# The ffn's base product by Strassen's scheme on two levels instead of one

## The chip, the cores and the metric

The kernel runs on one core of a Trainium2 chip. The metric is the device time of one execution in microseconds (us); a lower time is better. All data are float32.

## The reference

A transformer block for 32 sequences of 64 tokens, D = 1024. The parts with adapters are cut to what matters:

```python
x = x + attn(cond(x))               # cond: x @ W.T + a rank-32 adapter chosen by sequence
x = x + ffn(cond2(x))               # attn: 32 heads, 8 key/value heads, rotary, causal, w_o
def cond2(x):                       # 8 experts of rank 16, top 2
    return x @ W.T + 2 * experts2(x)
def ffn(y):                         # 8 experts of rank 16, top 2
    return y @ W_base.T + b_base + 2 * experts3(y)
```

Nothing nonlinear stands between the two dense products of cond2 and ffn but their gates, so the kernel multiplies the weights together once: the ffn's *base* is one product of x (1024 by 2048 tokens) with a combined matrix "cf" (1024 by 1024) that the kernel makes itself from W_base and cond2's W.

## The kernel before

Everything is kept transposed: features lie in the 128 partitions, tokens in the free dimension. Every large product is made by Strassen's scheme with Winograd's sums: a product of 2 x 2 blocks by seven block products `p1` to `p7` instead of eight. The class `Group` makes one such product for a pair of output chunks of 128 features. Its weights are three blocks of w ("11", "12", "22") and four sums s1 to s4 that GpSimd makes (`weight_sums`); its right sides are blocks of x and four sums t1 to t4 that VectorE makes (`column_sums`). Three PSUM banks x, y, z collect the seven products: p1 is copied out by ScalarE and then p2 goes on top in x, p6 and then p7 and p4 share y, p5 and then p3 share z; VectorE adds the parts on the way out. `mult` issues the matmuls of one product: 4 of 512 columns for a K half of 512.

The work goes in this order:

1. The *gen* stage makes the combined matrices: cq and ckv (kept in the scratch `cqkv`), then cf. For cf, `multiply("cf", ...)` goes through four groups; each makes four tiles of 128 x 512 that ScalarE's queue stores to the scratch `cffn`. Between its steps, a table `after` has other work done: the narrow columns (`narrow`), the rows of b2 (`low_rows`), and the sums of the attention's output weights w_o, which go to the scratch `wos`.
2. For each half `hf` of the tokens (1024): q and k, attention, the output projection, then the ffn.
3. The ffn: logits (`lgrows`, `lg`), gates, a product `h` for the experts' inner parts, the scaled inner parts `hw2` and `hw3`, and the base in four groups `ffn_pair(g)`. The experts' outer parts are added in PSUM: in the first group by `extra` (8 matmuls), in the others by one more matmul in each of the seven products (`tail`, over the sums `bs` and `th`).

In the gen stage the order on SP (loads), TensorE and VectorE is as written (`manual_schedule`, closed by `in_order.close()`); afterwards a scheduler orders the engines, but for parts that are marked again. Buffers come from pools: `wp` with two buffers each for the tags "w" (128 x 8 KB, a group's weights, `load_w` at line 404) and "s" (their sums), `tp` with eleven temporaries of 128 x 512, PSUM with three banks "bank" and five "ps". A tile's load waits until all that read the buffer's last tenant have finished.

```python
wp = ctx.enter_context(tc.tile_pool(name="wp", bufs=2))
tp = ctx.enter_context(tc.tile_pool(name="tp", bufs=11))
```

Of the kernel before, what the change touches and what calls it, by code (L numbers as in the profile page):

```python
# [76 lines left out]
def block_kernel(ctx: ExitStack, tc: tile.TileContext, a, out: bass.AP):  # L77
# [94 lines left out]
    def weight_sums(w, name, s=None):  # L172

        h = w.shape[1] // 2
        a11, a12 = w[:, :h, :P], w[:, h:, :P]
        a21, a22 = w[:, :h, P:], w[:, h:, P:]
        if s is None:
            s = wp.tile([P, 4, h, P], F32, tag="s", name=f"s_{name}")
        nc.gpsimd.tensor_add(s[:, 0], a21, a22)  # L179
        nc.gpsimd.tensor_sub(s[:, 1], s[:, 0], a11)  # L180
        nc.gpsimd.tensor_sub(s[:, 2], a11, a21)
        late["sums"] = nc.gpsimd.tensor_sub(s[:, 3], a12, s[:, 1])
        return s
# [34 lines left out]
    def columns(name, pool, b, n, h=H):  # L218
        tiles = [pool.tile([P, h, 512], F32, tag=f"sum{j}", name=f"sum{j}_{name}") for j in range(4)]
        return Columns(b, n, h, [[t[:, kc, :] for kc in range(h)] for t in tiles])  # L220
# [8 lines left out]
    class Group:  # L229
# [4 lines left out]
        def __init__(self, name, w, s, t, out, extra=None, known=None, bank=group_bank, late=False):  # L234
            self.name, self.out, self.extra, self.known, self.late = name, out, extra, known, late
            self.n, self.b, self.new = t.n, t.b, bank
            h = self.h = w.shape[1] // 2
            self.weights = {"11": w[:, :h, :P], "12": w[:, h:, :P], "22": w[:, h:, P:]}
            for j in range(4):
                self.weights[f"s{j + 1}"] = s[:, j]  # L240
# [13 lines left out]
        tail = None  # L254

        def mult(self, ps, left, right, first=False):
# [9 lines left out]
            if self.tail is not None:  # L266
                lhs, rhs = self.tail(left, right)
                nc.tensor.matmul(ps, lhs, rhs, start=False, stop=True, skip_group_check=True)
# [73 lines left out]
        def without_extra(self):  # L342

            for step in (self.p1, self.p6, self.p5, self.p7, self.p2, self.p4):
                step()

        def with_extra(self):
            self.more(self.z, 1, 1)
            self.out11()
            self.out00()  # L350
            self.p3()
            self.out10()
# [118 lines left out]
    cffn = scratch.tile([P, KC, NF], F32, tag="cffn", name="cffn")  # L471
    b1q = const.tile([P, NQ], F32, tag="b1q", name="b1q")
# [9 lines left out]
    with tc.tile_pool(name="gen", bufs=1) as gen:  # L482
# [56 lines left out]
        def multiply(name, inner, t, n, dst, at, diagonal=False, first=(), order=None, after={}):  # L539

            h = n // 2
            ws, groups = list(first), {}

            def load(g):
                while len(ws) <= min(g, 3):
                    ws.append(load_w(a[inner][len(ws)], f"{name}{len(ws)}"))

            def out(g, r, c, ps, add):
                o = tmp(f"{name}{g}{r}{c}")[:, :h]
# [4 lines left out]
                if diagonal and r == c:  # L554
                    d = o[:, g * P : (g + 1) * P]
                    nc.vector.tensor_add(d, d, ident)
                nc.scalar.dma_start(dst[:, g + r * H, at + c * h : at + (c + 1) * h], o)
# [112 lines left out]
        b2 = gen.tile([P, KC, P], F32, tag="w_os", name="b2")  # L670
        nc.sync.dma_start(b2, a["b2"])
        low_rows("b2f0", b2, w3, 512, b2s)

        def narrow(g, w):
            for r in range(2):
# [8 lines left out]
                nc.scalar.dma_start(cffn[:, g + r * H, D:], o)  # L684

            for n in range(2 * g, 2 * g + 2):
# [6 lines left out]

        multiply(
            "cf", "w2", t_cf, D, cffn, 0, diagonal=True,
            after={
                (0, "p1"): lambda w: low_rows("b2x", b2, w3x, NF - D, b2s[:, D:]),
                (0, "p7"): lambda w: low_rows("b2f1", b2, w3[:, :, 512:], 512, b2s[:, 512:]),
                (0, "p3"): lambda w: narrow(0, w),
                (1, "p4"): lambda w: narrow(1, w),  # L700
                (2, "p4"): lambda w: narrow(2, w),
                (3, "p4"): lambda w: narrow(3, w),
            },
        )

# [56 lines left out]
    def scaled(n, hf, h, gates):  # L762

        nm = f"r{n}_{hf}"
        both = hp.tile([P, TH], F32, tag="hw", name=f"hw{nm}")
        hw = [both[:, s * 512 : (s + 1) * 512] for s in range(NS)]
        for s in range(NS):
# [9 lines left out]
            nc.vector.tensor_mul(hw[s], h[s], gs)  # L777
# [5 lines left out]
    for hf in range(2):  # L783
# [15 lines left out]
        else:  # L799
# [3 lines left out]
            with tc.issue_after(late["third"].ins):  # L803
                tiles = [
                    gathered(hf, s, lambda name: a1[:, s * BS : (s + 1) * BS], BS) for s in range(NS)
                ]
            steps = [ranks(hf, s, x, tiles[s], low) for s in range(NS)]
# [30 lines left out]
        def qk_pair(g, z_bank=group_bank):  # L838
            w = load_w(cqkv[:, :, g * WG : (g + 1) * WG], f"qk{hf}{g}")
# [217 lines left out]
        with tc.manual_schedule():  # L1057
# [98 lines left out]
            xt = columns(f"y{hf}", scoped(f"sums_y{hf}", side="right"), x_half, 512)  # L1156
# [17 lines left out]
        bd = fp.tile([P, 2, P], F32, tag="bd", name=f"bd_{hf}")  # L1174
        bs = fp.tile([P, 4, 3, P], F32, tag="bs", name=f"bs_{hf}")
        th = fp.tile([P, 4, 512], F32, tag="th", name=f"th_{hf}")
        for kc in range(2, H):
            xt.make(kc)
        lg = ps_tile(f"lg_{hf}")
        for c in range(2):  # L1180
# [11 lines left out]
            nc.scalar.copy(rs, rows)  # L1192
            for i in range(4):
# [8 lines left out]
        lgv = lg[:, : NT * 2 * E].rearrange("p (t n e) -> p t n e", n=2, e=E)  # L1202
        lg3 = small(f"lg3_{hf}")
        nc.vector.tensor_copy(lg3, lgv[:, :, 1, :])
        gates2 = gates_of("2", hf, lgv[:, :, 0, :], lbias[:, hf * NT : (hf + 1) * NT, :])
# [14 lines left out]
        Group(f"h{hf}", w, weight_sums(w, f"h{hf}"), xt, out_h).early()  # L1220


        b2v, b3v = (b[:, :D].rearrange("p (g r o) -> p g r o", r=2, o=P) for b in (b2f, b3))
        for i, b in enumerate((b2v, b3v)):
            nc.gpsimd.tensor_sub(bd[:, i], b[:, 0, 0], b[:, 0, 1])
        nc.gpsimd.tensor_add(bs[:, 0], b2v[:, 1:, 1], b3v[:, 1:, 1])
        nc.gpsimd.tensor_sub(bs[:, 1], bs[:, 0], b2v[:, 1:, 0])
        nc.gpsimd.tensor_sub(bs[:, 2], b2v[:, 1:, 0], b2v[:, 1:, 1])
        nc.gpsimd.tensor_sub(bs[:, 3], b3v[:, 1:, 0], bs[:, 1])

        def ffn_pair(g):
            w = load_w(cffn[:, :, g * WG : (g + 1) * WG], f"f{hf}{g}")

            def out_f(r, c, ps, add):
                oc = 2 * g + r
                o = tmp(f"o_{hf}_{oc}_{c}")
                if add is None:
                    nc.scalar.activation(o, ps, AF.Identity, bias=bb[:, oc : oc + 1])
                else:
                    nc.vector.scalar_tensor_tensor(o, ps, bb[:, oc : oc + 1], add, ALU.add, ALU.add)  # L1240
                nc.scalar.dma_start(out[oc, :, hf, c, :], o)

            def extra(r, c):
                if (r, c) == (0, 1):
                    return [(bd[:, 0], hw2[1]), (bd[:, 1], hw3[1])]
                return [(b2v[:, 0, r], hw2[c]), (b3v[:, 0, r], hw3[c])]

            def tail(left, right):
                lhs = {"11": b2v[:, g, 0], "12": b3v[:, g, 0], "22": b3v[:, g, 1]}
                rhs = {"11": hw2[0], "21": hw3[0], "22": hw3[1]}  # L1250
                return (
                    bs[:, int(left[1]) - 1, g - 1] if left[0] == "s" else lhs[left],
                    th[:, int(right[1]) - 1] if right[0] == "t" else rhs[right],
                )

            s = weight_sums(w, f"f{hf}{g}")
            if g == 0:
                return Group(f"f{hf}{g}", w, s, xt, out_f, extra, late=True)
            group = Group(f"f{hf}{g}", w, s, xt, out_f)
            group.tail = tail  # L1260
            return group

        hw2 = scaled("2", hf, [h[0, c] for c in range(2)], gates2)
        ps = ps_tile(f"lgx_{hf}")
        for t in range(NT):
            nc.tensor.matmul(
                ps[:, t * E : (t + 1) * E],
                hw2[t // 4][:, t % 4 * P : (t % 4 + 1) * P],
                b2f[:, NF - E :],
                start=True,  # L1270
                stop=True,
            )
        gates3 = gates_of("3", hf, ps[:, : NT * E].rearrange("p (t e) -> p t e", e=E), lg3)
        for c in range(2):
            ps = ps_tile(f"hx_{hf}_{c}")
            nc.tensor.matmul(ps, b2f[:, D : D + P], hw2[c], start=True, stop=True)
            nc.vector.tensor_add(h[1, c], h[1, c], ps)
        first = ffn_pair(0)
        first.without_extra()
        hw3 = scaled("3", hf, [h[1, c] for c in range(2)], gates3)  # L1280
        first.with_extra()
        column_sums([th[:, j] for j in range(4)], lambda i, c: (hw2, hw3)[i][c], lambda t: t)
        for g in range(1, 4):
            group = ffn_pair(g)
            if g == 2:
                late["third"] = late["sums"]
            group.main()
# [89 lines left out]
```

## Time and profile before

| | us |
|---|---|
| median of 3 runs | 1213.21 (1212.85 to 1213.22) |
| the profiled execution | 1213.1 |
| its span, first to last instruction | 1211.3 |
| TensorE busy | 1203.2 |
| VectorE busy | 577.9 |
| GpSimd busy | 511.4 |
| ScalarE busy | 153.4 |

PE is TensorE's matmuls, PEld its weight loads, DVE VectorE, ACT ScalarE, POOL GpSimd, SP the engine that issues most loads; SPq and ACTq are DMAs issued there. A float32 matmul of the code appears as two records with a weight load each. A line such as `662.47 3.43 PE f_y L258 x8` of the chain reads: start, duration, engine, tile, line of the code, number of records. In the groups, "busy, mean ns | idle before, releaser" follow the shapes; a mean matmul record of 592 ns includes the drain, which overlaps the next one. Line 258 is `mult`, line 268 the `tail`, line 876 the v projection.

The stages by time: gen to about 296 us (cf from 176), q and k of the first half to 430, attention to 590, the ffn of the first half to 748, then the second half to 1211.

### The profile page before, as it was taken

The page shows a single profiled execution, that of the slowest core. Times are in us where ns is not written, and L with a number is a line of the kernel's source. Part 1 is how long each engine was busy: PE and PEld are TensorE (multiplying, and loading weights), DVE is VectorE, ACT ScalarE, POOL GpSimd, SP SyncE. Part 2 cuts the span into 40 slices and gives each one's busy share as a digit, 9 for nine tenths or more (in the row PEclk, how much of TensorE's full clock was granted, in tenths as well). Part 3 has the DMA queues.
Part 4 walks back from the last instruction along what each step waited for, and adds up shares of the span by engine and source line. Part 5 has one row for each costly group of instructions (what it writes and reads, how often), then busy time and mean ns, then how long its engine had stood idle before and what let it go on. Part 6 is the DMA issues. An engine that isn't in the chain of part 4 may idle for free.

```text
span 1211.3 us, 13619 instructions
## 1 busy us (share of the span) xinstructions
PE 1203.2 (99%) x5440; PEld 611.9 (51%) x5440; DVE 577.9 (48%) x941; ACT 153.4 (13%) x282; POOL 511.4 (42%) x437
## 2 busy tenths in 40 slices
PE   9999999999999999999999999999999999999998
PEld 3444874555444478544444444444468544444443
DVE  4312151115357789753941113456789764842111
ACT  1001000000001124320000000000224330000000
POOL 3341351443434746754723411532756653821010
PEclk9999999999999999999999999999999999999999
DMA  6553742645111111023112435111120124112110
GB/s 244 211 214 99 263 144 61 204 160 166 35 35 35 36 70 71 17 73 123 36 35 83 126 109 169 35 35 35 35 71 32 40 71 126 50 35 69 56 50 35
DMA packets 58992, 108.83 MB, mean 90 GB/s; under 512 B 5168, under 2 KB 35248, under 8 KB 57648
## 3 DMA queue, kind: packets, MB, share of 16 engines
q1 hardware_dynamic: 43136, 79.53, 19.7%
q10 hardware_dynamic: 13104, 20.03, 4.5%
q0 software_dynamic: 2688, 8.39, 2.1%
q8 instruction: 43, 0.70, 0.2%
q14 instruction: 21, 0.17, 0.0%
HBM read 83.72 MB, written 24.22 MB: 89 GB/s over the span
## 4 chain that ended last, share of the span: by engine, by line
PE 98%; DMA 1%; SPq 0%; DVE 0%; issue 0%
PE qk_y L258 9%; PE o_y L258 7%; PE f_y L258 7%; PE qk_x L258 6%; PE qk_z L258 6%; PE v L876 5%; PE f_z L258 5%; PE o_x L258 5%; PE f_x L258 5%; PE o_z L258 5%; PE cq_y L258 3%; PE cf_y L258 3%; PE sc L897 3%; PE pt L950 2%; PE cq_z L258 2%; PE cf_z L258 2%
## 5 line engine op out<-in xcount | busy, mean ns | idle before, releaser
L826 POOL TENSOR_TENSOR raw<-raw,consts 128x512 f32<-128x512 f32 x40 | 63.0, 1584 | 105.7 <-DVE t L825 105.7
L930 POOL TENSOR_TENSOR e<-e,top 128x512 f32<-128x512 f32 x64 | 64.9, 1042 | 57.3 <-DVE top L929 42.2
L942 POOL TENSOR_TENSOR e<-e,tot 128x512 f32<-128x512 f32 x64 | 66.1, 1064 | 27.3 <-DVE tot L940 27.3
L258 PE MATMUL qk_x<-x,w_qk 128*128 128x512 f32 x160 | 72.2, 594 | 0.0
L258 PE MATMUL qk_y<-sum_x,s_qk 128*128 128x512 f32 x160 | 72.2, 594 | 0.0
L179 POOL TENSOR_TENSOR s_f<-w_f 128x512 f32<-128x512 f32 x8 | 11.0, 1373 | 122.3 <-DMA w_f<-cffn 79.9
L258 PE MATMUL o_x<-q,w_o 128*128 128x512 f32 x128 | 58.9, 592 | 0.0
L876 PE MATMUL v<-w_v,x 128*128 128x256 f32 x256 | 58.7, 382 | 0.0
L258 PE MATMUL f_x<-x,w_f 128*128 128x512 f32 x128 | 57.9, 592 | 0.0
L258 PE MATMUL f_y<-sum_y,s_f 128*128 128x512 f32 x128 | 57.5, 592 | 0.0
L1051 POOL TENSOR_TENSOR x<-x,o_u 128x512 f32<-128x512 f32 x24 | 30.9, 1289 | 54.3 <-DVE o_u L1049 33.2
L876 PEld LDWEIGHTS v<-w_v,x 128*128 128x128 f32 x256 | 47.4, 190 | 8.4 <-issue 2.7
L258 PEld LDWEIGHTS qk_x<-x,w_qk 128*128 128x128 f32 x160 | 30.1, 190 | 38.0 <-issue 37.9
L827 DVE TENSOR_TENSOR t<-t,consts 128x512 f32<-128x512 f32 x40 | 48.7, 1230 | 0.7
L258 PEld LDWEIGHTS qk_y<-sum_x,s_qk 128*128 128x128 f32 x160 | 30.2, 190 | 37.1 <-issue 36.4
L179 POOL TENSOR_TENSOR s_qk<-w_qk 128x512 f32<-128x512 f32 x10 | 19.5, 1947 | 65.8 <-DMA w_qk<-cqkv 65.8
L939 DVE TENSOR_REDUCE tot<-e 128x8 f32<-128x512 f32 x64 | 40.5, 667 | 10.6 <-ACT e L934 10.4
L934 ACT ACTIVATE e<-e 128x512 f32<-128x512 f32 x64 | 38.2, 639 | 54.3 <-POOL e L930 54.2
L920 DVE TENSOR_TENSOR e<-sc,consts 128x512 f32<-128x512 f32 x64 | 39.7, 676 | 8.9 <-PE sc L897 8.9
L258 PEld LDWEIGHTS f_y<-sum_y,s_f 128*128 128x128 f32 x128 | 24.3, 190 | 30.6 <-issue 30.6
L258 PEld LDWEIGHTS f_x<-x,w_f 128*128 128x128 f32 x128 | 24.3, 190 | 30.6 <-issue 30.6
L836 DVE TENSOR_TENSOR q<-raw,t 128x512 f32<-128x512 f32 x32 | 38.4, 1205 | 2.5 <-POOL raw L826 2.3
(321 smaller groups left out, 2207.6 us busy)
## 6 DMA issues: line engine op xcount, KB each, us to landing
w_qk<-cqkv SPq DMA_DIRECT2D x10, 1024.0 KB, 5.5
x<-in_xT SPq DMA_DIRECT2D x16, 512.0 KB, 8.0
w_o<-in_wo SPq DMA_DIRECT2D x16, 512.0 KB, 4.7
s_o<-wos SPq DMA_DIRECT2D x16, 512.0 KB, 6.3
w_f<-cffn SPq DMA_DIRECT2D x8, 1024.0 KB, 5.5
outT<-o ACTq DMA_DIRECT2D x32, 256.0 KB, 2.9
cqkv<-cq ACTq DMA_DIRECT2D x16, 256.0 KB, 2.4
w_ckv<-in_w SPq DMA_DIRECT2D x4, 1024.0 KB, 5.4
```

Source lines behind the costliest of these rows:

```text
L258: nc.tensor.matmul(ps, self.weights[left][:, kc, :], self.right(right, kc), start=first and kc == 0, stop=kc == self.h - 1, skip_group_che ...
L826: nc.gpsimd.tensor_mul(rv, rv, c3)
L827: nc.vector.tensor_mul(t2v, t2v, s3)
L836: nc.vector.tensor_add(*unfinished.pop())
L876: nc.tensor.matmul(begun[t], x[kc][:, t * P : (t + 1) * P], wv[:, kc, :], start=False, stop=kc == KC - 1, skip_group_check=True,)
L897: nc.tensor.matmul(sc[j][:, n * S : (n + 1) * S], q[rows, g, b, 2 * mp : 2 * mp + 2, :].rearrange("p m t -> p (m t)"), k[rows, g, b, :], s ...
L920: nc.vector.tensor_add(per_key(e), per_key(sc[j]), mask.unsqueeze(1).to_broadcast([P, 8, S]))
L930: nc.gpsimd.tensor_sub(ev, ev, wide(top))
L934: nc.scalar.activation(e, e, AF.Exp, scale=SCALE)
L939: nc.vector.tensor_reduce(tot[:, i], es[i], AX.X, ALU.add)
L942: nc.gpsimd.tensor_mul(es[i], es[i], wide(tot[:, i]))
L1051: nc.gpsimd.tensor_add(xo, xo, to)
```

## The change

Each of the seven products of the base is itself made by seven products of *quarters*. Where the base was four groups with 512 x 512 blocks split once, it is now seven outer products (table `SEVEN`), each in two quarters (q = 0, 1), each quarter a `Quarter(Group)` with K halves of 256 (two matmuls a product) and 256 columns.

- The weights' sums of both levels are made once, in the gen stage, and kept in a scratch `cf7`: for each outer product seven blocks for each kappa (half of K) and q. A quarter loads its 14 blocks of 128 x 128 in one DMA into the tag "w". GpSimd's weight sums in the ffn's base are gone.
- cf's four groups run in the order 0, 2, 1, 3 of the output chunks and stay in SBUF (tile `cf`). `levels(kappa)` makes eleven steps (`level_one`: one of the outer sums, `level_two`: the inner sums of one outer block and its five stores on SP). Those of kappa 0 stand between the steps of the third group, on VectorE; those of kappa 1 after the last group, on VectorE and, for three blocks, on GpSimd.
- In the ffn the columns' inner sums (`inner_columns`) are made by VectorE in the tag "s". The outer level is added outside PSUM in accumulators a, b, c, z of 128 x 4 x 512: GpSimd adds the earlier accumulator to a quarter's parts (`known`), VectorE adds the result on the way out of PSUM.
- The experts' outer parts are now extra matmuls of 256 columns, eight in each quarter of p2, p5, p3 and p4. `tail`, `bs` and `th` are gone.
- The order on TensorE in the ffn is as written: of each quarter `begin` (p1, p6), then `finish` of the quarter before (p4, p3), then `middle` (p5, p2, p7, out11). The logits' second part, the gates' transposes and the `h` product are interleaved in a new order.
- In the gen stage the rows of b2 for columns 0 to 1023 move from before and inside cf to after it, the w_o sums are spread over cf's steps, the first qk weights are loaded inside cf, and the gathers for the second half are tied to two additions of GpSimd.

```diff
+    class Quarter(Group):
+        def sum(self, x):
+            if x != "u1":
+                self.pair = tmp(f"{self.name}_{x}")
+            at = self.n if x == "u1" else 0
+            return self.pair[:, at : at + self.n]
+        def begin(self):
+            self.p1()
+            self.p6()
+        def middle(self):
+            for step in (self.p5, self.p2, self.p7, self.out11):
                 step()
+        def end(self):
+            self.p4()
             self.p3()
+    SEVEN = (
+        *(("p1", "11", "11"), ("p6", "s2", "t2"), ("p2", "12", "21"), ("p7", "s3", "t3")),
+        *(("p5", "s1", "t1"), ("p3", "s4", "22"), ("p4", "22", "t4")),
+    )
+    PRIOR = {"p6": "a", "p2": "a", "p7": "b", "p3": "b", "p4": "c"}
+    KEPT = {"p1": "a", "p6": "b", "p7": "c", "p5": "z"}
+    OUT = {"p2": (0, 0), "p3": (0, 1), "p4": (1, 0), "p5": (1, 1)}
...
+    cf7 = scratch.tile([P, 7, 2, 2, 7, P], F32, tag="cf7", name="cf7")
...
+        def level_two(kappa, left, x, engine):
+            n = at_of[left]
...
+            engine.tensor_add(s[0][:, :, 0], a21, a22)
+            engine.tensor_sub(s[0][:, :, 1], s[0][:, :, 0], a11)
+            engine.tensor_sub(s[1][:, :, 0], a11, a21)
+            engine.tensor_sub(s[1][:, :, 1], a12, s[0][:, :, 1])
+            to = cf7[:, n, :, kappa]
+            for at, block in enumerate((a11, a12, a22)):
+                nc.sync.dma_start(to[:, :, at, :], block)
+            for i in range(2):
+                nc.sync.dma_start(
+                    to[:, :, 3 + 2 * i : 5 + 2 * i].rearrange("p q s o -> p q (s o)"),
+                    s[i].rearrange("p q s o -> p q (s o)"),
+                )
...
-        b2 = gen.tile([P, KC, P], F32, tag="w_os", name="b2")
+        b2 = hp.tile([P, TH], F32, tag="hw", name="b2").rearrange("p (k o) -> p k o", o=P)
         nc.sync.dma_start(b2, a["b2"])
-        low_rows("b2f0", b2, w3, 512, b2s)
...
+        for half in range(2):
+            at = slice(half * 512, (half + 1) * 512)
+            low_rows(f"b2f{half}", b2, w3[:, :, at], 512, b2s[:, at])
+        for step in levels(1, nc.gpsimd):
+            step()
...
+        def quarter(n, q):
+            step, _, _ = SEVEN[n]
+            w = wp.tile([P, KC, WG], F32, tag="w", name=f"w_f{hf}{n}{q}")
+            w = w.rearrange("p k o -> p (k o)")[:, : 14 * P].rearrange("p (k s o) -> p k s o", k=2, s=7)
+            nc.sync.dma_start(w, cf7[:, n, q])
...
+            def known(m, half, add):
+                if prior is not None:
+                    to = part(prior if kept is None else kept, m, half)
+                    late["sum"] = nc.gpsimd.tensor_add(to, part(prior, m, half), add)
...
-        for g in range(1, 4):
-            group = ffn_pair(g)
-            if g == 2:
-                late["third"] = late["sums"]
-            group.main()
+            for n in range(7):
...
+                for q in range(2):
...
+                    group = quarter(n, q)
+                    group.begin()
+                    if last is not None:
+                        finish(last)
+                    group.middle()
+                    if q == 0 and n < 6:
+                        ts[n + 1] = inner_columns(n + 1)
+                    last = group
...
+            finish(last)
```

## The prediction

> **What bounds the kernel now.** I read the page first: the engines' busy times and the chain that ended last.
>
> ```profile
> PE 1203.2 (99%) x5440; PEld 611.9 (51%) x5440; DVE 577.9 (48%) x941; ACT 153.4 (13%) x282; POOL 511.4 (42%) x437
> PE 98%; DMA 1%; SPq 0%; DVE 0%; issue 0%
> ```
>
> TensorE is busy in 99% of the span and is 98% of the chain; every other engine is at half or less. A matmul removed from the ffn is worth its full length, and every wait put on TensorE costs its full length. So I need two prices: a product, and a wait for weights. Next the chain in order of time, in the ffn of the first half, and in the v stage, which has matmuls of 256 columns.
>
> ```profile
> 662.47 3.43 PE f_y L258 x8
> 666.76 3.43 PE f_z L258 x8
> 671.05 3.43 PE f_y L258 x8
> ...
> 434.94 3.46 PE v L876 x16
> ```
>
> A matmul of the code gives two records. Four matmuls of 512 columns take 3.43 us, 0.858 us each; the next product starts 4.29 us after this one, and the 0.86 between is the tail (one matmul for the experts). Eight matmuls of 256 columns take 3.46 us, 0.4325 us each, so half the columns cost 50.4%. The groups by form show why weight loads don't spoil that:
>
> ```profile
> L876 PE MATMUL v<-w_v,x 128*128 128x256 f32 x256 | 58.7, 382 | 0.0
> L876 PEld LDWEIGHTS v<-w_v,x 128*128 128x128 f32 x256 | 47.4, 190 | 8.4 <-issue 2.7
> ```
>
> Two weight loads of 190 ns are 380 of the 432 ns. Last, SP's waits and the timeline around one weight load of the ffn:
>
> ```profile
> SPq L404 <- PE f_y L258: 167.1, 6, 39.9
> ...
> 615.58 3.70 PE L258 MATMUL h_y<-sum_y,w_h 128*128 128x512 f32 x8
> 619.11 3.60 PE L258 MATMUL h_z<-x,s_h 128*128 128x512 f32 x8
> 619.35 0.52 SPq L404 DMA_DIRECT2D w_f<-cffn  x1
> 624.97 1.51 POOL L179 TENSOR_TENSOR s_f<-w_f 128x512 f32<-128x512 f32 x1 [17.16 <-DMA w_f<-cffn]
> ...
> w_f<-cffn SPq DMA_DIRECT2D x8, 1024.0 KB, 5.5
> ```
>
> A load waits at SP until TensorE has done with the buffer's last tenant: the next product starts at 619.11, the load is issued at 619.35, its 1 MB is there 5.5 us later, its reader starts 0.12 after that. Nobody waits on TensorE, because the other of the two buffers holds a whole group, 7 x 4.29 = 30 us of work.
>
> **What the Trainium skill says.** "DMA: Bandwidth & Descriptors", section "Anatomy of one DMA", gives about 2.0 us plus bytes over 436 GB/s: 4.4 us for 1 MB. The trace has 5.4 to 5.8 (another queue than the page's fit), so I use the trace. "TensorE: Matmul & The Clock Gate", section "HAM oscillation", warns of idle gaps over about 3.4 us, after which the clock halves; in this trace the granted clock is 0.999 and there are no such gaps in the ffn. "SBUF — State Buffer", section "Who interferes with whom", says that VectorE operations with two SBUF inputs and GpSimd's reads shut each other out. The trace agrees: the same four sums beside GpSimd and without it are
>
> ```profile
> 165.13 5.58 DVE L191 TENSOR_TENSOR sum_cf<-w 128x512 f32<-128x512 f32 x4
> 170.64 2.48 DVE L193 TENSOR_TENSOR sum_cf<-w,sum_cf 128x512 f32<-128x512 f32 x4
> ```
>
> **The change, part by part.**
>
> *TensorE's work.* Before, per half: four groups x 28 matmuls plus 8 extras and 21 tails = 141 x 0.858 = 121.0 us (trace: 622.1 to 748.2 less about 5 us of small gate matmuls). After: 14 quarters x 14 = 196 matmuls of 256 columns, and 8 quarters (those of p2, p5, p3, p4) x 8 extras = 64: 260 x 0.4325 = 112.45 us. Saved: 8.6 per half, **17.1 us** in all.
>
> *The wait for weights.* The pool of w keeps two buffers. Quarter i+2 takes the buffer of quarter i, whose last reader is p3 in `finish`, and `finish(i)` stands behind `begin(i+1)`. What TensorE still has before `begin(i+2)` is then only: the two extras of p3 of i if it has extras (0.86 us), the six matmuls of `middle(i+1)` (2.60), and its four extras if it has them (1.73). So the cover is 2.60 to 5.19 us where it was some 30.
>
> The load is 14 x 64 KB = 917,504 bytes in runs of 7 KB a partition. No row shows it; it lies between the 512 KB loads of w_o, whose shortest is
>
> ```profile
> DMA to landing us min/median/max: 3.7/4.7/7.7
> ```
>
> and the 1 MB at 5.5. The isolated 1 MB load flows at about 385 GB/s in its middle; the 393 KB that ours has over w_o's take 1.0 at that: **4.7 us**, my estimate; bounds 4.4 and 5.5. With 0.24 to the issue, 0.1 to the reader and 0.2 for the exposed weight load (a product behind a wait takes 3.63 instead of 3.43), 5.25 us pass. The stall is 5.25 less cover, from the third quarter on. "Plain" is a quarter without extras:
> - 3 x cover 2.60 (two plain ones before it): 2.65 each, 7.95
> - 1 x cover 3.55 (the eight gate transposes, 0.95, help): 1.70
> - 2 x cover 4.33: 0.92 each, 1.84
> - 1 x cover 3.46: 1.79
> - 5 x cover 5.19: 0.06 each, 0.3
>
> 13.5 us per half, **27 us** in all. With 4.4 us it is 22; with 5.5 it is 46 (every term grows, the five small ones by 0.8). The first two quarters are covered by the h product and the gates. Output stores (256 KB, 2.9 us) run on the same DMA engines in quarters whose cover is just used up: +2.
>
> *The cf stage.* Its 16 stores of 256 KB become 70 stores (14 x (3 x 128 KB + 2 x 256 KB), 12.8 MB) on SP; at 0.33 to 0.42 us an issue, 35 of them are some 13 us of SP's time, twice, and the wo loads and the first qk load queue behind. cf's TensorE work is as before; the two rows of b2 (6.87 each) only move behind it. On VectorE the first kappa adds 8 sums of 512 (0.61) and 28 of 256 (0.36) = 15 us in group 2, which lasts 27.5 us and needs VectorE for 4; group 3's first eviction is another 14 us away. I cost that at nothing; the cover is that slack, and GpSimd's 11 us there eat into it. The second kappa is tighter: after the last eviction VectorE has 8 x 0.61 + 16 x 0.36 = 10.6 us, up to 19 if GpSimd's 12 operations of 0.68 shut it out, and only then the sums of x, which before started at once and just sufficed:
>
> ```profile
> 292.36 0.69 DVE L553 TENSOR_TENSOR cf<-cf_y,cf_p 128x512 f32<-128x512 f32 x1 [2.74 <-PE cf_y L258]
> 292.96 2.49 DVE L191 TENSOR_TENSOR sum_x<-x 128x512 f32<-128x512 f32 x4
> 302.99 0.69 DVE L288 TENSOR_TENSOR qk_u<-qk_y,qk_p 128x512 f32<-128x512 f32 x1 [0.31 <-issue]
> ```
>
> The moved b2 rows give 13.7 us more cover, plus some 3 that p5 leaves before p7 needs that eviction: about 17. Stall 0 to 3, I take +1.5; up to 8 if the eleven temporaries run out while stores drain.
>
> *Other engines in the ffn, costed at nothing.* GpSimd loses 16 sums of 1.3 (21 us a half) and gets 3 additions of 256 columns (0.7) in 10 quarters, 21 us. VectorE gets five or six evictions of 0.42 in each quarter and 3 to 4 us of inner sums in every second, under 5 of at least 6 us of TensorE. They hide behind TensorE; late, they would hold p3 and p7. The sixteen gathers for the second half (0.95 each) share GpSimd with these additions: 0 to 5 us, in the range only.
>
> *Sum.* The profiled execution took 1213.1 (span 1211.3 and 1.8 around it; the median of the runs is 1213.21, 0.1 higher). 1213.1 - 17.1 + 27 + 2 + 1.5 = 1226.5: **1226 us**.
>
> **The rivals.**
> - *A, the forecast: the weight wait outweighs the saved products.* For it: two buffers, SP's wait on TensorE, 5.5 us for 1 MB. 1216 to 1236. Chance 0.58.
> - *B, the loads are slower than I take them:* beside the stores, or the gathers (2.1 MB) and early x loads (4 MB) that SP puts ahead. For it: w_qk took up to 6.7 us beside a store. At 5.5 the stall is 46 us, at 6 about 58; stalls of over 3.4 us might then bring the clock down too. 1236 to 1262; chance 0.22.
> - *C, the other side: the loads are hidden and the products decide.* Its place is the same wait: all of it is covered if the load lands 2.1 us after its issue. Gain and loss are equal where these stalls sum to 17.1 - 2 - 1.5 = 13.6 instead of 27, which is at a landing of about 3.8 us. Against it: the smallest 512 KB load took 3.7. All hidden: 1196; more likely 1200 to 1210. Chance 0.15.
> - *D, they cancel:* a load of 3.8 us or partly covered stalls: 1213; chance 0.05.
> - That the quarters don't cost half is excluded by the v stage, unless waits keep weight loads from running ahead; that is in the upper end.
>
> **How the numbers follow.** A measurement of this kernel tells about 0.2%, 2.4 us, from no change. Faster is C, 0.15; same is D, 0.05; slower is A and B, 0.80. The range leaves out the better part of C below and the end of B above: 1206 to 1250; A's own is 1216 to 1236.
>
> **What would show it.** Right: TensorE's busy share falls visibly under 99% in both ffn stretches; the weight load of the quarters waits for a DMA from the new scratch, 2 to 3 us each at three quarters a half and little in those of p3 and p4; the matmul count of the ffn is 260 x 2 records a half with 0.43 us a pair; the load lands 4.4 to 5.5 us after issue. Wrong: no idle time at TensorE's weight loads there, or landings under 4 us, is C; idle time behind VectorE or GpSimd instead is a chain of additions that I cost at nothing; idle time between 290 and 320 us is the cf stage.

## The result, and the profile after

The changed kernel takes **1261.55 us** (median of 4 runs, 1260.45 to 1262.2) against 1213.22 for the kernel before on the same chip: 1.0398 times as long (95% interval 1.038 to 1.0416). It is slower, as forecast, but by 48 us where the forecast had 13, and outside the range of 1206 to 1250. The profiled execution took 1262.2, its span is 1260.4: 49.1 more than the span before.

From the page of the changed kernel: the engines, TensorE's granted clock in 40 slices, the chain that ended last by engine and by line, one group of matmuls, and the weight's load.

```profile
PE 1209.2 (96%) x5916; PEld 713.2 (57%) x5916; DVE 689.2 (55%) x1209; ACT 156.7 (12%) x302; POOL 541.5 (43%) x489
...
PEclk9999999998999999999999898999999999999999
...
PE 86%; DMA 11%; POOL 1%; DVE 1%; issue 0%; SPq 0%; DVEq 0%; POOLq 0%
...
L261 PE MATMUL f_x<-sum_y,w_f 128*128 128x256 f32 x128 | 37.0, 414 | 24.3 <-DMA w_f<-cf 24.3
...
w_f<-cf SPq DMA_DIRECT2D x28, 896.0 KB, 4.6
```

TensorE is no longer the whole chain: 11% of it is DMA. The f_x group waited 24.3 us for w_f, and the load lands after 4.6 us (median; the forecast took 4.7). Two things don't fit the forecast. TensorE's busy time *rose* by 6 us although the change removes 17.1 us of matmuls. And the PEclk line has eights where the page of before had none: the clock was halved at times.

The stages, from the start of the first matmul of one to that of the next, the last one to the end of the last matmul (from the timeline), with the best kernel that the experiments led to (e10, below) beside them:

| us | before | after | e10 |
|---|---|---|---|
| gen, up to the first qk | 295.86 | 297.44 | 296.52 |
| first qk stage | 133.61 | 145.36 | 136.89 |
| base of the first half and ranks, up to the second qk | 127.61 | 154.78 | 119.07 |
| second qk stage | 137.93 | 137.55 | 139.50 |
| base of the second half | 125.75 | 135.39 | 117.56 |

The attention and logit stages between them agree within 0.2 us in all three. So there are three places to look at: the two bases, the first qk stage, and the seam between the halves.

**The base.** TensorE's timeline in the first half (start, duration, line, tiles, records; in brackets the idle time before, and what ended it):

```profile
648.73 1.03 PE L261 MATMUL f_y<-s_f,w_f 128*128 128x256 f32 x4
652.42 1.13 PE L261 MATMUL f_x<-sum_y,w_f 128*128 128x256 f32 x4 [2.66 <-DMA w_f<-cf]
653.38 3.42 PE L261 MATMUL f_y<-s_f,w_f 128*128 128x256 f32 x8
656.60 1.23 PE L261 MATMUL f_z<-x,w_f 128*128 128x256 f32 x4
...
664.35 2.07 PE L261 MATMUL f_x<-sum_y,w_f 128*128 128x256 f32 x4 [3.06 <-DMA w_f<-cf]
```

The wait of 2.66 us at the third quarter is the one that the forecast has at 2.65. What follows it was not in the forecast: eight matmul records take 3.42 us instead of 1.89. In the records of the granted clock, a stretch of 3.41 us at half speed begins at 653.6. Such stretches follow most of the longer waits; up to the last matmul there are 41.0 us of them. TensorE stands still in 5.5 of these anyway, above all before the first qk stage; in the other 35.5 it gets half as much done, which costs **17.7 us**.

**The first qk stage.** TensorE, then VectorE, in the same kernel:

```profile
297.44 3.60 PE L261 MATMUL qk_x<-x,w_qk 128*128 128x512 f32 x8
309.48 3.75 PE L261 MATMUL qk_z<-sum_x,s_qk 128*128 128x512 f32 x4 [8.44 <-DVE sum_x L191]
```

```profile
287.70 0.69 DVE L736 TENSOR_TENSOR cfs<-cf 128x512 f32<-128x512 f32 x1 [2.81 <-issue]
293.53 1.74 DVE L736 TENSOR_TENSOR cfs<-cf 128x512 f32<-128x512 f32 x1 [5.13 <-DMA b2s<-b2f0o]
300.39 0.69 DVE L736 TENSOR_TENSOR cfs<-cf,cfs 128x512 f32<-128x512 f32 x1 [5.12 <-DMA cf<-cft]
```

TensorE stands still for 8.44 us until the sums of x come, and those stand on VectorE behind the sums of the second kappa. VectorE isn't busy but waits, twice for over 5 us, each time for the store that frees a temporary: one of the rows of b2, one of cf's sums. From 305.42 on, still inside the gap, the clock is at half for 10.24 us; 6.2 of them are work, which costs 3.1 us on top of the 8.44.

**The seam between the halves.** GpSimd, and TensorE's last quarter:

```profile
779.23 1.26 POOL L179 TENSOR_TENSOR s_qk<-w_qk 128x512 f32<-128x512 f32 x1 [8.75 <-DMA w_qk<-cqkv]
780.45 1.26 POOL L181 TENSOR_TENSOR s_qk<-w_qk 128x512 f32<-128x512 f32 x1
781.67 1.26 POOL L180 TENSOR_TENSOR s_qk<-s_qk,w_qk 128x512 f32<-128x512 f32 x1
782.89 0.72 POOL L1399 TENSOR_TENSOR c_f<-c_f,f_u 128x256 f32<-128x256 f32 x1
```

```profile
784.19 2.07 PE L261 MATMUL f_z<-sum_y,w_f 128*128 128x256 f32 x4 [4.45 <-DVE o L1415]
```

Three weight sums of the next half, which had to wait for their weights, stand ahead of the last of the additions by `known`. VectorE's o needs that addition, and p3 needs the bank that o empties: 4.45 us, then 6.83 us at half clock.

### The profile page after: what moved, and what is told of

Same layout as the page of the kernel before. It is cut to its first block, busy times and chain, and to the rows that moved or that the text cites. A ratio compares the mean times of both kernels' runs of the same rounds, so it can differ in the third digit from the quotient of the medians.

```text
span 1260.4 us, 15112 instructions
## 1 busy us (share of the span) xinstructions
PE 1209.2 (96%) x5916; PEld 713.2 (57%) x5916; DVE 689.2 (55%) x1209; ACT 156.7 (12%) x302; POOL 541.5 (43%) x489
## 4 chain that ended last, share of the span: by engine, by line
PE 86%; DMA 11%; POOL 1%; DVE 1%; issue 0%; SPq 0%; DVEq 0%; POOLq 0%
DMA w_f<-cf 9%; PE qk_y L261 8%; PE o_y L261 7%; PE qk_z L261 6%; PE qk_x L261 5%; PE f_y L261 5%; PE v L996 5%; PE o_x L261 4%; PE o_z L261 4%; PE cf_y L261 3%; PE cq_y L261 3%; PE f_x L261 3%; PE f_z L261 2%; PE sc L1017 2%; PE pt L1070 2%; PE cq_z L261 2%
## 5 line engine op out<-in xcount | busy, mean ns | idle before, releaser
L261 PE MATMUL f_y<-s_f,w_f 128*128 128x256 f32 x336 | 91.2, 411 | 0.5 <-DVE f_u L300 0.5
L261 PEld LDWEIGHTS f_y<-s_f,w_f 128*128 128x128 f32 x336 | 70.2, 209 | 12.4 <-DVE f_u L300 0.9
L261 PE MATMUL f_x<-sum_y,w_f 128*128 128x256 f32 x128 | 37.0, 414 | 24.3 <-DMA w_f<-cf 24.3
L1059 DVE TENSOR_REDUCE tot<-e 128x8 f32<-128x512 f32 x64 | 40.5, 667 | 10.6 <-ACT e L1054 10.4
L261 PE MATMUL qk_z<-sum_x,s_qk 128*128 128x512 f32 x80 | 38.2, 620 | 8.4 <-DVE sum_x L191 8.4
L261 PEld LDWEIGHTS f_x<-sum_y,w_f 128*128 128x128 f32 x128 | 23.8, 196 | 33.1 <-DMA w_f<-cf 30.4
L1049 DVE TENSOR_REDUCE top<-e 128x8 f32<-128x512 f32 x64 | 39.6, 674 | 0.0
```

What stands on the lines that cost most here:

```text
L261: nc.tensor.matmul(ps, self.weights[left][:, kc, :], self.right(right, kc), start=first and kc == 0, stop=kc == self.h - 1, skip_group_che ...
L1049: nc.vector.tensor_reduce(top, ev, AX.X, ALU.max)
L1059: nc.vector.tensor_reduce(tot[:, i], es[i], AX.X, ALU.add)
```

## The experiments

Twelve kernels ran, all variants of the changed kernel. "Before" in their comparisons is 1212.85 to 1213.51 (medians). Numbers of a single execution are from the profiled one; in e1, e3, e4, e5, e6 and e9 that was the fastest of the four runs.

**e1: sums of the last columns ahead of the rows of b2.**

```
+        for step in levels(1, nc.gpsimd):
+            step()
         for half in range(2):
             low_rows(f"b2f{half}", ...)
-        for step in levels(1, nc.gpsimd):
-            step()
```

> The changed kernel, with the eleven steps of the second kappa written ahead of the two rows of b2 instead of behind them; TensorE's order is the same, only the order in which temporaries are taken differs. Theory (the rows' two temporaries, given back only after TensorE, ScalarE and a store, hold VectorE's sums up): the 8.4 us gap of TensorE before the first qk sums and most of the 10 us at half clock behind it go, 1261.5 - 8 to 12 = 1250 to 1254. Rival (VectorE and GpSimd shut each other out, the sums are simply too long): the gap stays within 2 us of 8.4, 1259 to 1262.

Measured: 1254.95 us, ratio 1.0349 (1.0332 to 1.0367), just above the 1250 to 1254 expected. The qk stage fell from 145.36 to 139.53 us, its half clock from 10.24 to 3.41. So the temporaries that the rows of b2 held are most of that gap; about 6 us against the stage before remain.

**e2: a third weight buffer.**

```
-            w = wp.tile([P, KC, WG], F32, tag="w", ...)
+            third = (2 * n + q) % 3 == 2
+            w = (fp if third else wp).tile([P, KC, WG], F32, tag="w3" if third else "w", ...)
```

> The changed kernel, with a third buffer for the quarters' weights (one quarter in three takes its tile from the ffn's pool). Theory (two buffers give too little cover for a 4.6 us load): TensorE's waits for the new scratch, 19 us in the first half and 14 in the second, fall under 3 us in all, and the half-clock stretches inside the quarters go with them: 1261.5 - 30 - 8 to 12 = 1219 to 1224. Rival (the rate of the loads, the stores and the gathers is the limit): waits of over 10 us a half stay, 1245 or more. Rival (VectorE's and GpSimd's additions take the place): the waits on DMA go, but idle time behind DVE or POOL of as much comes, 1245 or more.

Measured: 1232.73 us, ratio 1.0159 (1.0142 to 1.0176); expected were 1219 to 1224. Every wait for w_f is gone, and the base of the second half takes 117.56 us, 8.19 less than before: the quarters do save what the forecast says. But the buffer lies where the next half's q comes, so the sixteen gathers into q now stood behind the whole first half, and its ranks waited for them one by one:

```profile
762.02 0.44 PE L459 MATMUL h<-x,q 128*32 128x64 f32 x8 [3.66 <-DMA q<-in_a,rows_of]
762.80 0.44 PE L459 MATMUL h<-x,q 128*32 128x64 f32 x8 [0.34 <-DMA q<-in_a,rows_of]
763.59 0.44 PE L459 MATMUL h<-x,q 128*32 128x64 f32 x8 [0.35 <-DMA q<-in_a,rows_of]
```

Work in such scraps kept the clock at half for 30.72 us. A wait removed had made another transfer late.

**e3: matmuls that nobody reads, in the longest waits.** They stand behind `middle` of quarters (0,1), (1,0), (1,1), (3,0), (3,1).

```
                     group.middle()
+                    if (n, q) in ((0, 1), (1, 0), (1, 1), (3, 0), (3, 1)):
+                        for _ in range(4):
+                            nc.tensor.matmul(fill[:, :256], ident, xt.whole[0][:, 0, :256], ...)
```

> The changed kernel, with four matmuls of 256 columns on other data, read by nobody, behind the middle of the quarters (0,1), (1,0), (1,1), (3,0), (3,1) of each half: 1.73 us each, where TensorE stood idle for 2.1 to 3.4 us. Theory (a gap of 2 us and more brings the granted clock to half for 3.4 us, which costs 1.7 us a time): the granted clock in the quarters goes back to 1.0 but for the gaps at the ends, 4 to 6 stretches fewer, 1261.5 - 7 to 11 = 1251 to 1255. Rival (the half clock is only a reading, or it hides in waiting): 1260 to 1263; or slower by up to 10 x 1.7 = 17 us if the added matmuls are not covered.

Measured: 1250.99 us (1248.98 to 1258.99), ratio 1.0333 (1.0295 to 1.037), 10.6 *faster* with 40 matmuls more. In the profile, no stretch at half clock is left in the base of either half but the one behind the gap at the seam. So the clock is a cost of its own, beside the wait.

**e4: weights loaded for the first two quarters only**; the other twelve of each half multiply with these again, so this leaves out part of the computation.

```
+            if n == 0:
+                loaded[q] = wp.tile([P, KC, WG], F32, tag="w", ...)
+            w = loaded[q]
...
-            nc.sync.dma_start(w, cf7[:, n, q])
+            if n == 0:
+                nc.sync.dma_start(w, cf7[:, n, q])
```

> The changed kernel, with only the first two quarters of each half loading weights; the other twelve use those again (the product is then not the ffn's, the work of every engine else is the same). Theory: as with the third buffer or up to 3 us less, 1216 to 1222: what is left over the kernel before is the gap before qk (8.4 + its half clock), the gap of 4.5 at the end of the first half, and 1.6, against 17.1 saved. Rival (additions of VectorE and GpSimd bound the quarters): 1240 or more.

Measured: 1221.8 us, ratio 1.0072 (1.0055 to 1.0089). The base of the second half takes 117.56 us, as with three buffers. Even without these loads the kernel is slower than before, by the first qk stage (144.36 us) and by two gaps of the first half, 4.2 us in its middle and 4.3 at the seam, each with 6.83 us at half clock behind it.

**e5: the weight sums behind the last addition.**

```
-        pair = qk_pair(4)
+        if hf == 0:
+            pair = qk_pair(4)
+        else:
+            with tc.issue_after(late["sum"].ins):
+                pair = qk_pair(4)
```

> One edit to the changed kernel: on GpSimd, the weight sums of the next half's first qk pair stand behind the last known addition (c_f) of the first half's ffn instead of three of them ahead of it. Theory (in the changed kernel that addition ran at 782.89 only because three sums waiting for w_qk until 779.23 stood ahead of it, and VectorE's o and TensorE's p3 waited for it): the gap of 4.5 us ahead of f_z at the end of the first half goes, and with it most of the 6.83 us at half clock that followed it, 3.4 us: 1253 to 1257 from 1261.5. Rival (p3 waits for a free temporary or for VectorE itself, and the addition is only the last of several): the gap stays within 1 us of 4.5 and the time at 1260 to 1262.

Measured: 1259.68 us (1254.92 to 1260.82), ratio 1.0383 (1.0366 to 1.0401). In the profile, the 1254.92 run, the gap of 4.45 us and the half clock behind it are gone, so GpSimd's order is the cause of that gap. The median fell by only 1.9 us where 4.5 to 8.5 were expected. The second half of the same profile has 10.24 us at half clock instead of 6.83, without any change there: how much half clock a set of waits brings varies from run to run (last section).

**e6: the next half's x behind the weights on SP.**

```
+            with ExitStack() as behind:
+                if hf == 1:
+                    behind.enter_context(tc.issue_after(late[f"w_f{(4, 6)[kc // H]}"].ins))
                 nc.sync.dma_start(t[kc], a["xT"][kc, :, hf * TH : (hf + 1) * TH])
...
-            nc.sync.dma_start(w, cf7[:, n, q])
+            late[f"w_f{n}"] = nc.sync.dma_start(w, cf7[:, n, q])
```

> One edit to the changed kernel: on SP, the next half's x loads stand behind the first half's w_f loads of the fifth product (x of the first four chunks) and of the seventh (the other four) instead of ahead of the third, fourth and the last ones. Theory (the x loads held up the quarters' weights in the first half, which is why its waits for w_f came to 19 us and the second half's to 13.5): the waits of the first half fall to 13 to 15 us, the stretches at half clock in its quarters from 17 us to 7 to 10, and the time to 1252 to 1257; x is still there for the ranks, or late by up to 3 us. Rival (the gathers, the output stores or the clock itself make the difference between the halves): waits of the first half stay at 18 to 20 us and the time at 1260 to 1264.

Measured: 1254.48 us, ratio 1.0343 (1.0326 to 1.0361). The waits for w_f in the first half's quarters, from matmul starts (some 0.17 us a wait more than in the brackets, because a record's time includes the drain), fell from 19.0 to 14.5 us, the second half's stayed (13.1 and 13.4); half clock in the first half's quarters from 17.06 to 6.83. The x loads ahead in SP's queue are what made the first half worse.

**e7: e1, e5 and a third buffer that lets the gathers come during the base.** The buffer gets a pool on the side of the next half's attention, and q is split so that only the half that is filled late lies there.

> Three edits to the changed kernel together: a third weight buffer, kept in memory that the next half's attention fills late, so that the gathers come during the last quarters of the first half instead of after them; the second level's sums of the last columns of cf ahead of the two rows of b2; the weight sums behind the last known addition. Theory (the quarters do save the 17.1 us of the forecast, and all that was lost on top is waits for weights, for temporaries and for GpSimd's order, with the half clock that follows each): no wait for w_f; ffn of the second half 117.6 us; first half's end without the gaps of 4.2 us and without the 3.7 us waits of the ranks; what stays is 6 to 7 us at the first qk stage and in the generation. Time 1200 to 1206, 0.6 to 1.1 per cent below the kernel before. Rival (the eight gathers or the next half's loads now collide with something else at the boundary and bring back a gap and the half clock): 1210 to 1220.

Measured: 1212.06 us, ratio 0.9993 (0.9986 to 0.9999). The rival was right: the gathers now ran between the last quarters, twelve of the sixteen in a row on GpSimd ahead of an addition that TensorE needed:

```profile
725.48 1.05 POOL L440 DMA_INDIRECT q<-in_a,rows_of  x1 [0.15 <-issue]
...
739.39 0.95 POOL L440 DMA_INDIRECT q<-in_a,rows_of  x1 [0.30 <-issue]
740.36 0.74 POOL L1412 TENSOR_TENSOR c_f<-c_f,f_u 128x256 f32<-128x256 f32 x1
```

```profile
741.66 2.08 PE L261 MATMUL f_z<-sum_y,w_f 128*128 128x256 f32 x4 [6.45 <-DVE o L1428]
```

**e8: the same, with the halves of q in pools of their own**, so that the gathers stand on GpSimd where the changed kernel has them.

> The same edits as in the run with three weight buffers and early gathers, with one more: the two halves of q lie in pools of their own, so that the sixteen gathers stand on GpSimd where the changed kernel has them (ahead of the first and behind the last addition of the fourth product) instead of between the last quarters, where they held up the addition c_f until 740.36 and TensorE for 6.6 us. Theory (with the weights, the temporaries and GpSimd's order out of the way only the quarters' saving and some 6 us at the first qk stage are left): the 6.6 us gap and the 6.83 us at half clock behind it go, 9 to 10 us: 1201 to 1204 from 1212.1, ratio to before 0.990 to 0.993. Rival (the next half's loads of x and of w_qk or the ranks take the place of the gathers as the late one at the half boundary): 1207 to 1212.

Measured: 1209.83 us, ratio 0.997 (0.9959 to 0.9981); expected were 1201 to 1204. The seam is clean, but the first eight gathers now do the same harm further up, which in the changed kernel lay under a wait for w_f:

```profile
687.67 1.13 PE L261 MATMUL f_z<-sum_y,w_f 128*128 128x256 f32 x4 [4.22 <-DVE c_f L1421]
```

**e9: these eight gathers four by four**, in the pauses of the two quarters of p2.

```
+                        behind.enter_context(tc.issue_after(late[f"gather{2 * s + b // 4}"].ins))
...
                     group.begin()
+                    if n == 2:
+                        late[f"gather{q}"] = late["sum"]
```

> The run with the gathers in place, with one more edit: the first eight gathers stand four by four in the 7 us in which GpSimd has nothing to add in the two quarters of the third product, instead of eight in a row (10.5 us) ahead of the fourth product's first additions, where TensorE waited 4.22 us for VectorE's c_f and VectorE 5.87 us for GpSimd's. Theory (GpSimd's order is the limit there): the gap of 4.4 us and the 3.41 us at half clock behind it go, 6 us: 1203 to 1205 from 1209.8. Rival (the chain of VectorE and GpSimd is late there for another reason, or a gather of four makes another addition late): 1207 to 1211.

Measured: 1203.58 us, ratio 0.9921 (0.99 to 0.9941). In the profile (the run of 1202.29) the gap is gone and no half clock is left between the cf stage and the end of the matmuls. With four gathers (mostly 0.95 us each, 1.25 apart) in each of these pauses GpSimd's additions are in time. The other eight still run in a row, from 686.95 to 696.77, where no addition is due, and TensorE waits for nothing there: what counts is what stands behind the gathers, not their number.

**e10: second-level sums in an order that frees the first-level sums early** (in `levels(1)`: sums 1, 2, 4, 3, each used up before the next).

> The run with the gathers spread, with one more edit: the second level's sums of cf's last columns are made in an order that frees each first-level sum as soon as it is used, so that fewer of the eleven temporaries are held at a time. Theory (at the start of the first qk stage VectorE stood still for 6.16 us in the middle of these sums, for want of a free temporary, and TensorE's waits for sum_x of 3.3 us, two re-orderings and 3.41 us at half clock come from it): VectorE's pause shrinks below 2 us and the qk stage from 139.7 us by 3 to 5 us; time 1199 to 1202. Rival (the stores of cf's sums, not their number at a time, set when temporaries come free): the pause and the stage stay within 1 us, and the time within 1 us of the run without this edit.

Measured: **1200.9 us** (1200.79 to 1201.21), ratio **0.9892** (0.9876 to 0.9909). The time came out as expected, the reason didn't: VectorE's pause is still 5.55 us where it was 6.16, as the rival has it.

```profile
291.10 2.80 DVE L739 TENSOR_TENSOR cfs<-cf,cfs 128x512 f32<-128x512 f32 x2 [5.55 <-POOL s_qk L179]
```

The line names GpSimd as what ended the pause, but VectorE also waits there for a store of cf's second-level sums (cft), which frees a temporary. That store was issued at 284.30, right behind the 1 MB load of the first qk weights on SP, and landed 6.7 us later, at 290.98, 0.12 ahead of VectorE; in e1 and e9, too, it lands 0.12 ahead. So the queue behind the large load is the likely cause of the pause; no run tests it. The stage lost 1.36 us of its 138.25; with another order of VectorE's sums and of TensorE's products, one gap of 1.09 us is left where there were three (1.62, 0.89 and 1.25, from matmul starts).

```profile
PE 1188.3 (99%) x5916; PEld 704.5 (59%) x5916; DVE 699.7 (58%) x1209; ACT 156.5 (13%) x302; POOL 538.6 (45%) x489
...
PEclk9999999999999999999999999999999999999999
...
PE 96%; DMA 2%; POOL 0%; issue 0%; SPq 0%; DVE 0%; ACT 0%; ACTq 0%; POOLq 0%
```

With the same 5916 matmul records as the changed kernel TensorE is busy for 20.9 us less; 17.7 of them are the half clock. VectorE and GpSimd do the same work as there and hold up almost nothing.

**e11 and e12: two weight buffers again, everything else as in e10; e12 with the matmuls of e3.** They take the cost of the buffers apart.

> The best run so far (1200.9 us: sums first and in the shorter order, sums behind the last addition, gathers spread, three weight buffers) with the third weight buffer taken away again, so that a weight's load starts only when the quarter two before it has ended, as in the changed kernel. Theory (with all else in place the two buffers alone cost the waits for w_f, 27 to 28 us in both halves as the forecast and the second half of the changed kernel have it, and the half clock that they bring on top, 7 to 14 us at half clock in each half): 1235 to 1241. Rival (most of the 60 us between the changed kernel and the best run came from the gathers, the temporaries and GpSimd's order, and the buffers only moved with them): 1215 to 1228.

> The run with two weight buffers again, with four matmuls whose result nothing reads behind the middle steps of five of the fourteen quarters, where the waits for w_f are longest: the load still lands when it did, but TensorE isn't idle for over 2 us. Theory (the waits alone are worth the forecast's 27 us, the rest is the clock): no stretch at half clock in the ffn, 1227 to 1231, which is 5 to 12 below the same kernel without them. Rival (stretches at half clock don't come from the idle time): time within 2 us of the run without them, or above.

Measured: e11 **1249.39 us**, ratio 1.0294 (1.0276 to 1.0311); e12 **1237.25 us**, ratio 1.02 (1.0183 to 1.0217). The third buffer alone is worth 48.5 us of the 60.7 between the changed kernel and e10, more than the 34 to 40 expected. In e11's profile the two bases are 28.0 and 20.4 us longer than in e10, with 30.7 us of half clock, which costs 15.0 us of the 48.4; the waits for w_f come to 31.6, from matmul starts. One wait in e11, and the same place in e12:

```profile
696.75 2.02 PE L261 MATMUL f_x<-sum_y,w_f 128*128 128x256 f32 x4 [2.00 <-DMA w_f<-cf]
698.56 2.73 PE L261 MATMUL f_y<-s_f,w_f 128*128 128x256 f32 x8
```

```profile
688.88 1.89 PE L1520 MATMUL fill<-sum_y,consts 128*128 128x256 f32 x8
691.04 1.13 PE L261 MATMUL f_x<-sum_y,w_f 128*128 128x256 f32 x4 [0.27 <-DMA w_f<-cf]
692.00 1.89 PE L261 MATMUL f_y<-s_f,w_f 128*128 128x256 f32 x8
```

Four matmuls take 1.73 us of a wait that was there anyway, and the next product runs at full clock. In all they take 12.1 us off. e12 missed its range of 1227 to 1231: the fill costs 8.65 us a half (20 x 0.4325), not all of it inside waits, and 3.41 us at half clock are left.

## Why the prediction was right or wrong

The direction and the mechanism were right, Rival A's: two buffers, a wait at TensorE's weights, more than the saved products are worth. The forecast's sum was off by 35.7 us (49.1 of span against 13.4). Its terms:

- *TensorE's work, -17.1:* right, 16.7. Without waits the base of the second half takes 117.56 us against 125.75, -8.2, and that of the first 119.07 against 127.61, -8.5 (e10).
- *The load, 4.7 us:* right; it landed after 4.4, 4.6 and 7.5 us (shortest, median, longest).
- *The waits, +27:* right for the second half (13.1 us from matmul starts, forecast 13.5), too small for the first: 19.0. The forecast had the x loads that SP puts ahead under Rival B and not in the sum; e6 shows them to be the cause of 4.5 of the 5.5 us.
- *Output stores, +2:* not seen; the second half's waits come out without them.
- *The clock, +0:* the step that failed most, **17.7 us**. The forecast took from the Trainium skill, "TensorE: Matmul & The Clock Gate", section "HAM oscillation", that idle gaps of over about 3.4 us matter, saw that its own stalls were 2.65 at most, and put the clock into Rival B only. Here waits of 2.1 us already did it, 2.0 in the profile's bracket (e11 above); the measurement decides. e3 and e12 show the cost by itself.
- *The cf stage, +1.5:* too small; 11.75 in the stage, of which 3.1 is half clock and 8.44 the gap. The forecast named the cause ("up to 8 if the eleven temporaries run out while stores drain") and then took the cheap end. The rows of b2, counted there as 13.7 us of *cover*, were what held the temporaries (e1). Without the half clock the stage was 7.2 us over the forecast. Gen took 1.6 more on top.
- *VectorE's and GpSimd's chain in the ffn, +0:* wrong at the seam, 4.5 us, and hidden elsewhere. The forecast weighed these engines by their busy time, which does fit. What it left out is the order on GpSimd: three sums that wait for w_qk, or eight gathers in a row, ahead of one addition of 0.72 us (e5, e7 to e9). The gathers were in its range only, at 0 to 5 us.

So 17.7 + 5.5 - 2 + 7.2 + 1.6 + 4.5, about 34.5 of the 35.7. Rival B's range, 1236 to 1262, holds the result with its clock and its x loads, though not for its main reason, slow loads: the median landing was 4.6 us. Rival C's other side exists, but by a third buffer instead of faster loads: 1200.9 us, near the 1196 given for "all hidden".

## What to carry to other kernels

Cutting a product into smaller pieces shortens the cover of each load: count what the tensor engine still has to do between the release of a buffer and its next use, and add a buffer before the pieces. Count a wait of over 2 us on the tensor engine as the wait plus 1.7 us of half clock, as it cost here where it fell into one window (last section), and treat the order on a helper engine as a cost even where its busy time fits: one small operation behind a queue of waiting ones can hold the whole chain. When a wait is taken out, look again at what it hid; here three further limits came up one after another (e2, e7, e8).

## What the runs showed of the hardware

**The clock is decided by windows of 3.41 us, and 60% of idle time in one is enough.** In every profile that has several stretches at half clock they start on one grid of 3.4133 us, within 0.01 us. The Trainium skill, "TensorE: Matmul & The Clock Gate", section "What's actually happening", has such a window of 3413 ns that runs freely, and an idle window as the condition for half clock. I laid each profile's grid over TensorE's idle times, counted from matmul starts as in e6 (from 130 us on, eleven kernels with such stretches), and took the windows at full clock with over 1 us of idle time:

| idle time in the window | windows | next one at half clock |
|---|---|---|
| 1.0 to 2.03 us | 51 | 0 |
| 2.03 to 2.2 us | 18 | 15 |
| 2.2 us and more | 33 | 33 |

So half clock comes after some 2.1 us of idle time, 60% of a window and not a whole one. A wait of 2.1 us does it only if it lies inside one window; e8's gap of 4.4 us, split into 2.16 and 2.22 by the edge of a window, brought one stretch and not two.

The way back is stricter. Of the 73 windows at half clock 45 had at most 0.43 us of idle time, and full clock followed each of them; 24 had 0.65 us or more, and half clock followed each of them; of the four between, three went back. So one window at half clock is the price only if the work behind the wait is dense: the scraps of e2 kept the clock down for nine windows, the 8.44 us of the qk stage for three.

As the grid doesn't start with the program, the same waits bring more or less of it from run to run. That fits the spread of the times: 5.9 us between the four runs of e5, whose longer waits of 2.1 to 3.6 us lie at this limit, and 0.4 us in e10, which has none of over 1.9. In e9, too, no single wait is over 1.9, but the gaps of the qk stage bring one window to 2.07; its runs lie 3.6 us apart. That it is the cause of the spread is argued, not shown.
